# A graph convolution with a mixture of experts on one core: the loads of x placed by hand, and token gathers that run ahead by tiles

## The chip, the cores and the metric

The kernel runs on one core of one Trainium2 chip. The metric is the time of one execution in device microseconds. Each kernel is run several times, and the median is compared.

## The reference, cut to what matters

There are 12500 nodes of 256 features, 212500 edges sorted by destination (200000 drawn ones and a loop for each node), and 64 experts.

```python
h = feats * rsqrt(deg_out)[:, None]
m = segment_sum(h[src], dst, num_segments=n) * rsqrt(deg_in)[:, None]
x = (m @ W_gc + b_gc) + (feats @ W_res + b_res)
# top-2 of 64 experts: the two largest of x @ Wg + bg, softmax of the two
# each expert: gelu(tokens @ w1 + b1) @ w2 + b2, 256 -> 512 -> 256, capacity 1024
core = zeros((N, D)).at[tok].add(gate[:, None] * expert_output)
y = x + core
y = (y - mean(y, 0)) * rsqrt(var(y, 0) + eps) * gamma + beta   # over the nodes
out = layernorm(feats + y)                                      # over the features
```

## The kernel before, in words

The execution has five stretches. Up to about 400 us the degrees of the nodes are counted. Around 400 to 440 us the scaled features go to memory as h_d. From there to about 2605 us runs the graph stage: 1416 rows of up to 128 edges, each with one indirect transfer on POOL that gathers 128 rows of h_d (line L962) and one product with a 0/1 matrix on PE (L976). Work for groups of finished nodes (their products with the weights, the routing, the stores) is put into this loop at chosen rows: `at_row(t, f)` files f in a heap named todo, and after row c everything due by then is written into the program. At about 2640 us the experts begin, and they end near 3428 us. Then the batch norm and the layer norm follow, until 3577 us.

Three arrays in memory join the stages. x2_d (x_d in the trace) holds for each node its 256 features and its two gate values, and the experts gather tokens from it. z_d holds x, and the experts add their outputs to it by indirect transfers that accumulate. Afterwards the norms read z_d. The helper `by_rows` stores both: L1148 for whole groups, L1152 for the ragged end, whose source is a corner of the tile rel.

Twenty "early" tiles of tokens go through their experts inside the graph stage, on gaps of PE. `sort_early` and `early_tile` lay out their index tables, `gate_tile` writes their outputs into the tile acc, and `add_early` (L1562) adds an output to z_d. Eight of these adds (AT_ONCE) are issued right behind the last row of the graph stage, before what is left in todo; the other twelve are given to chosen parts of the experts (adds_at), where `gather` issues one in the middle of a part's gathers. Their row numbers come from at_e in the first case, and from a copy named taken_at in the second.

The experts' tokens are laid out as 73 parts of at most four tiles of 128 tokens: 219 tiles in all. `parts` is a fixed order. Some experts share an output product with their neighbour (`pair_at`). For part q:

- `begin` copies the expert's slice of the index tables (`sort_slots`, the copy L2118 and its companion), loads its weights (L1884, 1 MB) and its bias (L1886) on the queue of SP, and issues the gathers of its tokens from x2_d (L1931) on POOL.
- `turn` transposes the tokens on PE (L1947, xtp) and copies them to xT on DVE (L1951).
- `hidden` makes the first product (L1960, hp) and the gelu on ACT (L1964).
- `gates_of` (DVE) takes the gate values from the gathered rows (L1975).
- `outputs` makes the second product (L1983, yp), DVE adds the bias and scales by the gate (L1987 and L1988, yo), and POOL adds the tile to z_d (L1993).

There are 16 buffers for gathered tiles (xg), 10 for outputs (yo), 4 for weights, two for xT.

What sets the order: inside `manual_schedule` the instructions of the engines named (PE and DVE) keep the order of the program, while those of the others are placed by a scheduler. All transfers of POOL, gathers and adds, are chained in the order of the program by `in_order`. Gathers are asked for three parts ahead:

```python
if q not in pair_at and q + AHEAD < len(parts):
    begin(q + AHEAD)
if q + 1 < len(parts):
    xT = turned(q + 1)
```

The adds of one expert go to different nodes and don't wait for each other. Those of the next expert may hit the same nodes, so each waits in `landed` until every add of the group before has landed:

```python
if group != adding["group"]:
    adding.update(group=group, before=adding["these"], these=[])
for before in adding["before"]:
    tc.add_manual_dep(st.ins, before.ins.name, ...Sync...)
```

The early adds form groups of one. The final norms need x again. Its 14 pieces (LOADS, twelve of them 1 MB) are loaded on SP by the line L2151, which stands in the loop over the parts at every fourth part from part 6 on; the scheduler decides when SP issues them, as soon as their place in the tile acc is free by its reckoning, so that in the trace they start at 2030 us already. At the very end the norms load z_d (L2227) once the last add has landed.

Of the kernel before, what the change touches and what calls it, by code (L numbers as in the profile page):

```python
# [8 lines left out]
F32 = mybir.dt.float32  # L9
# [96 lines left out]
SORT_AT, TAKE_AT, STEP, AT_ONCE = 710, 796, 27, 8  # L106
# [38 lines left out]
def gnn_moe_kernel(  # L145
# [698 lines left out]
    with ExitStack() as stack:  # L844
# [274 lines left out]
        def nodes(t0, n, t):  # L1119
# [25 lines left out]
            def by_rows(to, of):  # L1145

                k = n if not last else 2
                st = [nc.sync.dma_start(  # L1148
                    to[t0 * P : (t0 + k) * P].rearrange("(t p) d -> p t d", p=P), of[:, :k]
                )]  # L1150
                if last:
                    st.append(nc.sync.dma_start(to[(t0 + k) * P : N], of[:RAG, k]))  # L1152
# [243 lines left out]
        xg_e = [xg_e, acc[:, NP + 19 * D : NP + 19 * D + D2]]  # L1396
        e_regs = {}
# [69 lines left out]
        def early_tile(i, t):  # L1467
# [20 lines left out]
            V.tensor_copy(at_e[:, :, i : i + 1], T3[:, :2, of])  # L1488
            V.tensor_copy(snd_e[:, i : i + 1], T3[:, 2, of])
# [213 lines left out]

        BATCH = 9
# [69 lines left out]
        with tc.manual_schedule(engines={  # L1774
# [18 lines left out]
            at_row(SORT_AT, sort_early)  # L1793
            at_row(TAKE_AT - 16, lambda t: soon.update(close=True))
# [38 lines left out]
    with ExitStack() as stack:  # L1833
# [33 lines left out]
        taken_at = route.tile([P, EARLY], I32)  # L1867
        V.tensor_copy(taken_at, at_e[:, 1])
# [3 lines left out]
    with ExitStack() as stack:  # L1872
# [6 lines left out]
        REGS, YO, COLS = 4, 10, RPE - 1  # L1879
        assert max(TOKENS) * TU <= COLS * P  # L1880

        def load(e):
            w = wp.tile([P, WROW], F32, name="w")
            nc.sync.dma_start(w, wpack[bass.ds(e, 1)].rearrange("a p f -> p (a f)"))  # L1884
# [35 lines left out]
        def gather(at, m, q=None):  # L1920

            xg = []
            for k in range(0, m, P):
                if k // P == -(-m // P) // 2 and q in adds_at:
                    st = add_early(adds_at[q], taken_at)
# [11 lines left out]
                in_order(i)  # L1937
                xg.append(g[:r])
# [136 lines left out]
        x_loads = LOADS[:7] + LOADS[9:] + LOADS[7:9]  # L2075
        large = [q for q in range(AHEAD, 6 + 4 * len(x_loads[:-2])) if parts[q][2] > 2 * P]
# [5 lines left out]
        def begin(q):  # L2082
            i, b, m = parts[q]
            if i not in given:
                if i not in columns_of:
                    n = 1
                    at = order.index(i)
                    while n < REGS and order[at : at + n + 1] == [*range(i, i + n + 1)]:
                        n += 1
                    _, regs = nc.values_load_multi_w_load_instructions(  # L2090
                        exp_row[0:1, i : i + n],
                        engines=[SP],
                        min_val=0,
                        max_val=E - 1,
                        skip_runtime_bounds_check_because="exp_row is an order of the experts",
                    )
                    _, columns = nc.values_load_multi_w_load_instructions(
                        exp8_row[0:1, i : i + n],
                        engines=[DVE],
                        min_val=0,  # L2100
                        max_val=(E - 1) * RPE + 1,
                        skip_runtime_bounds_check_because="exp8_row is an order of the experts",
                    )
                    for k in range(n):
                        columns_of[i + k], reg_of[i + k] = columns[k], regs[k]
                sort_slots(i, 0)
                if q >= AHEAD:
                    sort_slots(i, 1)
                given[i] = load(reg_of[i])
            xg[q] = gather(table(q), m, q)  # L2110
# [24 lines left out]
        with tc.manual_schedule(engines={mybir.EngineType.PE, DVE}):  # L2135
            for q in range(AHEAD):
                begin(q)
            V.scalar_tensor_tensor(free, node, 0.0, spread, op0=ALU.is_equal, op1=ALU.mult)
            V.tensor_tensor(slot[:, 1], free, slot[:, 0], op=ALU.add)
            for i in sorted({parts[q][0] for q in range(AHEAD)}):  # L2140
                sort_slots(i, 1)
            xT = turned(0)
            for q, (i, b, m) in enumerate(parts):
                if q >= 6 and q % 4 == 2 and (q - 6) // 4 < len(LOADS):
                    t0, n = x_loads[(q - 6) // 4]
# [7 lines left out]
                if q not in pair_at and q + AHEAD < len(parts):  # L2153
                    begin(q + AHEAD)
                if q + 1 < len(parts):
                    xT = turned(q + 1)
                mine = (*given[i], table(q), gates(q), h1, m, f"expert{i}")
                if q in pair_at:
                    rest = pair_of_outputs([kept.pop(pair_at[q]), mine])
                    begin(q + AHEAD)  # L2160
# [7 lines left out]
                else:  # L2168
                    outputs(*mine)
                if q == 16:  # L2170
# [227 lines left out]
```

## Time and profile before

| | us |
|---|---|
| three timed runs | 3569.35, 3597.57, 3601.11 |
| their median | 3597.57 |
| the profiled execution, its own time | 3578.71 |
| its span in the profile | 3576.9 |
| PE busy | 2494.7 (70%) |
| POOL busy | 2186.7 (61%) |
| DVE busy | 1797.0 (50%) |
| ACT busy | 826.2 (23%) |

The mean granted clock of PE is 0.821 over the span. The core moved 562.31 MB, 157 GB/s on the mean.

How to read it. Busy times are sums over stretches with different limits, so the share of an engine says little by itself. An instruction row gives its start, its duration in us, the engine, the line, the operation, output and inputs, and in brackets how long the engine was idle before it and what ended that idle time ("issue" where the profile shows nothing that it waited for). "SPq" rows are SP's own instructions that issue a transfer, and their duration contains the time they were held. A row of waits reads: total us, how many times, mean us. A row of groups has a count, the busy time and the mean in ns of one, then the idle time before them and what ended most of it. A row of stretches gives for each engine its busy time and its instructions, then the granted clock of PE, the share of time in which the transfer engines were busy, and GB/s.

### The profile page before, as it was taken

The page shows a single profiled execution, that of the slowest core. Times are in us where ns is not written, and L with a number is a line of the kernel's source. Part 1 is how long each engine was busy: PE and PEld are TensorE (multiplying, and loading weights), DVE is VectorE, ACT ScalarE, POOL GpSimd, SP SyncE. Part 2 cuts the span into 40 slices and gives each one's busy share as a digit, 9 for nine tenths or more (in the row PEclk, how much of TensorE's full clock was granted, in tenths as well). Part 3 has the DMA queues.
Part 4 walks back from the last instruction along what each step waited for, and adds up shares of the span by engine and source line. Part 5 has one row for each costly group of instructions (what it writes and reads, how often), then busy time and mean ns, then how long its engine had stood idle before and what let it go on. Part 6 is the DMA issues. An engine that isn't in the chain of part 4 may idle for free. (4 is left out here: it accounts for less than half of the span.)

```text
span 3576.9 us, 40976 instructions
## 1 busy us (share of the span) xinstructions
PE 2494.7 (70%) x12046; PEld 1898.2 (53%) x12121; DVE 1797.0 (50%) x7367; ACT 826.2 (23%) x2028; POOL 2186.7 (61%) x2169
## 2 busy tenths in 40 slices
PE   2626066566666667676676666578769999999966
PEld 1515033455555545555555455456547767767756
DVE  2829554255455555655455444356643333334347
ACT  1515301122112122121222112122112211211246
POOL 6270777666666666666665666666547777777621
PEclk6657567788787878788788787788889999999988
DMA  7370853455455554555554544445466667667764
GB/s 258 109 235 4 304 191 110 144 146 152 130 144 143 147 142 139 146 140 162 162 162 145 162 152 137 138 144 179 132 171 148 162 150 193 161 173 183 174 168 144
DMA packets 319779, 562.31 MB, mean 157 GB/s; under 512 B 47850, under 2 KB 236366, under 8 KB 308798
## 3 DMA queue, kind: packets, MB, share of 16 engines
q0 software_dynamic: 119456, 266.90, 29.4%
q1 hardware_dynamic: 186555, 279.83, 24.5%
q10 hardware_dynamic: 13539, 12.90, 1.2%
q8 instruction: 99, 1.62, 0.2%
q14 instruction: 130, 1.06, 0.1%
HBM read 455.41 MB, written 105.12 MB: 157 GB/s over the span
## 5 line engine op out<-in xcount | busy, mean ns | idle before, releaser
L962 POOL DMA_INDIRECT ring<-h_d,src_col x1416 | 1364.4, 964 | 748.1 <-issue 385.4
L976 PE MATMUL p<-ring,o 128*128 128x258 f32 x2832 | 899.3, 447 | 175.0 <-DMA ring<-h_d,src_col 97.1
L976 PEld LDWEIGHTS p<-ring,o 128*128 128x128 f32 x2832 | 594.7, 223 | 337.3 <-issue 148.0
L954 DVE TENSOR_SCALAR o<-lane,rel 128x128 f32<-128x128 f32 x1416 | 356.4, 298 | 328.6 <-remote 163.8
L1993 POOL DMA_INDIRECT z_d<-yo,tables x219 | 340.5, 1555 | 146.2 <-issue 48.9
L1983 PE MATMUL yp<-w,h 128*128 128x256 f32 (+7 forms) x1928 | 381.2, 392 | 9.4 <-DVE yo L1987 8.4
L1960 PE MATMUL hp<-xT,w 128*128 128x384 f32 (+22 forms) x1168 | 350.5, 454 | 2.0 <-DVE xT L1951 1.3
L1983 PEld LDWEIGHTS yp<-w,h 128*128 128x128 f32 (+7 forms) x1928 | 296.3, 174 | 71.3 <-issue 17.2
L1964 ACT ACTIVATE h<-hp,w 128x384 f32<-128x384 f32 (+21 forms) x292 | 159.1, 546 | 622.8 <-PE hp L1960 513.7
L1960 PEld LDWEIGHTS hp<-xT,w 128*128 128x128 f32 x1168 | 218.6, 192 | 112.3 <-issue 49.6
L1931 POOL DMA_INDIRECT xg<-x_d,tables x219 | 215.3, 983 | 77.9 <-issue 52.1
L1951 DVE COPY xT<-xtp 128x768 f32<-128x768 f32 (+20 forms) x73 | 63.6, 871 | 329.6 <-PE xtp L1947 295.5
L1755 ACT ACTIVATE again<-again,factor 128x256 f32<-128x256 f32 x180 | 82.4, 502 | 634.2 <-issue 364.3
L309 POOL DMA_INDIRECT early<-in_x,src_col x140 | 149.8, 1070 | 113.4 <-DMA early_d<-early 60.8
L1051 PE MATMUL q<-ident,s 128*128 128x128 f32 x236 | 58.8, 339 | 200.7 <-DVE tables L1738 72.8
L1010 ACT COPY s<-p 128x258 f32<-128x258 f32 x118 | 44.0, 373 | 636.8 <-remote 274.1
L1730 PE MATMUL q<-r_out,tables 128*128 128x98 f32 x360 | 70.1, 327 | 160.0 <-DVE tables L1738 59.0
L591 PE MATMUL deg<-o_hi,o_lo 128*128 128x98 bf16 x1254 | 105.8, 255 | 102.8 <-issue 66.0
L1987 DVE TENSOR_TENSOR yo<-yp,bb 128x256 f32<-128x256 f32 (+6 forms) x219 | 92.9, 424 | 162.5 <-PE yp L1983 132.4
L589 ACT ACTIVATE s_lo<-lane_b,nb 128x128 bf16<-128x128 bf16 x396 | 122.1, 388 | 201.6 <-PE deg_s L593 96.0
L1730 PEld LDWEIGHTS q<-r_out,tables 128*128 128x128 f32 x360 | 65.7, 238 | 177.3 <-issue 74.4
L1051 PEld LDWEIGHTS q<-ident,s 128*128 128x128 f32 x236 | 35.2, 171 | 234.4 <-DVE tables L1738 79.5
(428 smaller groups left out, 3853.0 us busy)
## 6 DMA issues: line engine op xcount, KB each, us to landing
w<-in_wpack SPq DMA_DIRECT2D x64, 1026.0 KB
again<-early_d SPq DMA_DIRECT2D x90, 256.0 KB
ring<-h_d,src_col POOLq DMA_INDIRECT x1416
acc<-in_wpack SPq DMA_DIRECT2D x20, 1026.0 KB
early_d<-early SPq DMA_DIRECT2D x70, 256.0 KB
tables<-h_d SPq DMA_DIRECT2D x104, 128.0 KB
acc<-acc_d SPq DMA_DIRECT2D x14, 896.0 KB
acc<-in_x SPq DMA_DIRECT2D x12, 1024.0 KB
```

Source lines behind the costliest of these rows:

```text
L309: GP.indirect_dma_start(out=t[:, c % 2], out_offset=None, in_=x, in_offset=bass.IndirectOffsetOnAxis(ap=src_col[:, MC + c : MC + c + 1], a ...
L589: S.activation(s_lo[:, i], lane_b, AF.Sign, bias=nb[:, k - k0, i : i + 1])
L591: T.matmul(deg, o_lo[:, i], o_hi[:, i], start=c + i == 0, stop=False)
L954: o_last[u] = V.tensor_scalar(o_of[u][:, j], lane, rel[:, c : c + 1], None, op0=ALU.is_equal)
L962: i = GP.indirect_dma_start(out=r[:, k, :D], out_offset=None, in_=h_d, in_offset=bass.IndirectOffsetOnAxis(ap=src_col[:, c : c + 1], axis=0),)
L976: i = T.matmul(p_of[g], o_of[v][:, n], r[:, k], start=j == 0, stop=j == GR - 1)
L1730: T.matmul(p_r[:, i], wide[:, i * P : (i + 1) * P], r_out, start=True, stop=True)
L1931: i = GP.indirect_dma_start(out=g[:r], out_offset=None, in_=x2_d, in_offset=bass.IndirectOffsetOnAxis(ap=at[:r, 0, k : k + 1], axis=0),)
L1960: T.matmul(hp[:, :m], w1[:, c, j * P : (j + 1) * P], xT[:, c, :m], start=c == 0, stop=c == 1,)
L1964: S.activation(h1[:, j, :m], hp[:, :m], AF.Gelu, bias=w[:, 2 * H + 4 * D + j : 2 * H + 4 * D + j + 1],)
L1983: T.matmul(yp, h1[:, j, a : a + r], w2[:, j], start=j == 0, stop=j == 3)
L1993: st = GP.indirect_dma_start(out=z_d, out_offset=bass.IndirectOffsetOnAxis(ap=at[:r, 1, k : k + 1], axis=0), in_=yo, in_offset=None, compu ...
```

## The change

It has five parts.

1. *The stores at the end of the graph stage.* Seven early adds (AT_ONCE) stand there in place of eight, so thirteen are given to parts of the experts. The late stores of z_d are declared free of a conflict with these adds, as the adds already were with the stores: the adds are a no-dep group now, and the stores name it. The adds still wait for each other.
2. *The row numbers of early tiles.* A table at_all in acc gets the row numbers of each early tile by one more copy in `early_tile` (20 in all, each with an offset from a register). It replaces at_e[:, 1] and the copy taken_at after the graph stage.
3. *The loads of x.* SP is in the manual schedule of the experts, so it keeps the order of the program there. Six pieces are loaded at chosen rows of the graph stage, four behind the last work of todo, and four in the experts, at parts 10, 20, 50 and 54.
4. *Gathers and weights.* `begin` is split: weights are loaded up to three parts ahead as before; gathers run ahead as long as the tiles from part q on fit into XG = 20 buffers (16 before), at most two parts in one call. Index tables are laid out with the gathers. The weights of the second expert wait for the first gather.
5. *Part 1.* Its tokens are transposed after the outputs of part 0, and no longer ahead of them.

In the built order of the changed kernel the matrix products and ACT's work are those of before, in the same order, but for part 5.

```diff
-SORT_AT, TAKE_AT, STEP, AT_ONCE = 710, 796, 27, 8
+SORT_AT, TAKE_AT, STEP, AT_ONCE = 710, 796, 27, 7
...
                 if soon.get("ranked", NT) <= t0 and to is z_d:
                     for i in st:
                         tc.add_to_no_dep_group("late stores", i.ins)
+                        tc.declare_no_dep(
+                            i.ins,
+                            group="early adds",
+                            reason="nodes of early tiles were ranked before",
+                        )
                         late_stores.append(i)
...
+        a = yo_at[-1] + D
+        at_all = acc[:, a : a + EARLY].bitcast(I32)
...
             V.tensor_copy(at_e[:, :, i : i + 1], T3[:, :2, of])
+            V.tensor_copy(at_all[:, i : i + 1], T3[:, 1, of])
...
+        def load_x(j):
+            t0, n = LOADS[j]
+            r = rows(t0)
+            nc.sync.dma_start(xs[:r, t0 : t0 + n], part_of(x, t0, n))
...
+            for j, r in ((9, 1090), (3, 1130), (4, 1330), (0, 1385), (1, 1390), (2, 1395)):
+                at_row(r, lambda t, j=j: load_x(j))
...
             for i in range(AT_ONCE):
+                st = add_early(i, at_all)
+                tc.add_to_no_dep_group("early adds", st.ins)
                 tc.declare_no_dep(
-                    add_early(i, at_e[:, 1]).ins,
+                    st.ins,
...
             while todo:
                 t, _, f = heapq.heappop(todo)
                 f(t)
+            for j in (5, 11, 12, 13):
+                load_x(j)
...
-        taken_at = route.tile([P, EARLY], I32)
-        V.tensor_copy(taken_at, at_e[:, 1])
...
         def load(e):
             w = wp.tile([P, WROW], F32, name="w")
-            nc.sync.dma_start(w, wpack[bass.ds(e, 1)].rearrange("a p f -> p (a f)"))
+            i = nc.sync.dma_start(w, wpack[bass.ds(e, 1)].rearrange("a p f -> p (a f)"))
+            if len(first) == 1:
+                sync(i, first[0])
+                first.append(i)
...
-                g = two.tile([P, D2], F32, name="xg", bufs=16)
+                g = two.tile([P, D2], F32, name="xg", bufs=XG)
...
-        x_loads = LOADS[:7] + LOADS[9:] + LOADS[7:9]
-        large = [q for q in range(AHEAD, 6 + 4 * len(x_loads[:-2])) if parts[q][2] > 2 * P]
+        tiles_of = [-(-m // P) for _, _, m in parts]
+        x_at = {10: LOADS[10], 20: LOADS[6], 50: LOADS[7], 54: LOADS[8]}
+        large = [q for q in range(AHEAD, 50 - AHEAD) if parts[q][2] > 2 * P]
...
+        def begin(q, which=1):
+
+            to = min(q + AHEAD, len(parts) - 1)
+            most = fetched[0] + 2 if which else AHEAD
+            while True:
+                p = fetched[0]
+                if loaded[0] <= to and (loaded[0] <= p or p >= most):
+                    i = parts[loaded[0]][0]
+                    names(i)
+                    if i not in given:
+                        given[i] = load(reg_of[i])
+                    loaded[0] += 1
+                elif p < min(most, len(parts)) and sum(tiles_of[max(q, 0) : p + 1]) <= XG:
+                    i, b, m = parts[p]
+                    names(i)
+                    if i not in laid:
+                        sort_slots(i, 0)
+                        if which:
+                            sort_slots(i, 1)
+                        laid.append(i)
+                    xg[p] = gather(table(p), m, p)
+                    fetched[0] += 1
+                elif loaded[0] > to:
+                    break
+                else:
+                    most = p
...
-        with tc.manual_schedule(engines={mybir.EngineType.PE, DVE}):
-            for q in range(AHEAD):
-                begin(q)
+        with tc.manual_schedule(engines={mybir.EngineType.PE, DVE, SP}):
+            begin(-1, 0)
...
-                if q >= 6 and q % 4 == 2 and (q - 6) // 4 < len(LOADS):
-                    t0, n = x_loads[(q - 6) // 4]
+                if q in x_at:
+                    t0, n = x_at[q]
...
-                if q not in pair_at and q + AHEAD < len(parts):
-                    begin(q + AHEAD)
-                if q + 1 < len(parts):
+                if q not in pair_at:
+                    begin(q)
+                if 0 < q < len(parts) - 1:
                     xT = turned(q + 1)
...
+                if q == 0:
+                    xT = turned(1)
```

More of the change, by code (lines that the diff above doesn't have):

```diff
@@ L1924, in gather @@
                 if k // P == -(-m // P) // 2 and q in adds_at:
-                    st = add_early(adds_at[q], taken_at)
+                    st = add_early(adds_at[q], at_all)
                     landed(st, f"early{adds_at[q]}")
@@ L1937, in gather @@
                 in_order(i)
+                if not first:
+                    first.append(i)
                 xg.append(g[:r])
@@ L2080, in gnn_moe_kernel @@
         xg, given = {}, {}
[L2082 to L2110, printed above, removed]
@@ new lines, in gnn_moe_kernel, with names @@
+        loaded, fetched = [0], [0]
+        def names(i):
+            if i in columns_of:
+                return
+            n = 1
+            at = order.index(i)
+            while n < REGS and order[at : at + n + 1] == [*range(i, i + n + 1)]:
+                n += 1
+            _, regs = nc.values_load_multi_w_load_instructions(
+                exp_row[0:1, i : i + n],
+                engines=[SP],
+                min_val=0,
+                max_val=E - 1,
+                skip_runtime_bounds_check_because="exp_row is an order of the experts",
+            )
+            _, columns = nc.values_load_multi_w_load_instructions(
+                exp8_row[0:1, i : i + n],
+                engines=[DVE],
+                min_val=0,
+                max_val=(E - 1) * RPE + 1,
+                skip_runtime_bounds_check_because="exp8_row is an order of the experts",
+            )
+            for k in range(n):
+                columns_of[i + k], reg_of[i + k] = columns[k], regs[k]
```

8 lines of the change are left out of this document (5 added, 3 removed).

## The prediction

> **What bounds the kernel now.** I read the stretches of the span first, because the change touches only the hand-over from the graph stage to the experts and the experts themselves.
>
> ```profile
> span 3576.9 us, 40976 instructions
> core 0: us, PE busy (x) PEld busy (x) DVE busy (x) ACT busy (x) POOL busy (x), PEclk, DMA share, GB/s
> 2640.00:2720.00 80.00, 78.80 (x408) 61.04 (x409) 29.76 (x92) 19.00 (x37) 48.33 (x38) 0.97 0.65 162
> 2720.00:3280.00 560.00, 531.57 (x2489) 392.06 (x2489) 208.40 (x684) 110.78 (x203) 409.38 (x321) 0.98 0.70 168
> 3280.00:3440.00 160.00, 148.47 (x636) 109.80 (x634) 56.37 (x172) 32.11 (x56) 109.04 (x84) 0.98 0.65 146
> ```
>
> The experts run from about 2640 to 3440 us. In the middle 560 us PE is busy 95% at a granted clock of 0.98, so matrix work sets the pace and only 28 us are idle there. POOL is nearly as full: 409.4 us busy, and behind each of its 321 indirect transfers stands a gap of 0.30 us (rows below), another 96 us. That leaves POOL 54 us of real waiting in 560. Two engines are close to full, and PE's idle time is what a better order could win.
>
> ```profile
> PE xtp L1947 <- DMA xg<-x_d,tables: 18.2, 17, 2.4
> PE yp L1983 <- DVE yo L1987: 8.4, 3, 3.2
> PE hp L1960 <- DVE xT L1951: 1.3, 1, 1.3
> ```
>
> These are PE's waits between 2640 and 3430 us: 18.2 us for gathered tokens (xg, late 17 times), 8.4 us for DVE's outputs. Then the hand-over, from the lists in order of time on SP, POOL, DVE and PE:
>
> ```profile
> 2601.28 15.33 SPq L2151 DMA_DIRECT2D acc<-in_x  x2
> 2623.01 0.37 SPq L1148 DMA_DIRECT2D z_d<-rel  x1
> 2625.36 0.44 SPq L1152 DMA_DIRECT2D x_d<-rel  x1
> 2628.51 0.37 SPq L1884 DMA_DIRECT2D w<-in_wpack  x1
> 2584.99 1.87 POOL L1562 DMA_INDIRECT z_d<-acc,rel  x1 [0.30 <-issue]
> 2612.36 1.55 POOL L1562 DMA_INDIRECT z_d<-acc,rel  x1 [3.01 <-DMA z_d<-acc,rel]
> 2616.39 1.71 POOL L1562 DMA_INDIRECT z_d<-acc,rel  x1 [2.47 <-DMA z_d<-acc,rel]
> 2629.35 1.02 POOL L1931 DMA_INDIRECT xg<-x_d,tables  x1 [11.25 <-issue]
> 2609.64 0.15 DVE L1268 SCALAR_TENSOR_TENSOR rel<-src_col 128x3 f32<-128x3 f32 x1
> 2618.24 0.20 DVE L1864 CAST exp_row<-ord_p 1x64 int32<-1x64 f32 x1
> 2621.12 0.17 DVE L2118 COPY tables<-tables 128x7 int32 x1
> 2637.94 0.66 PE L1947 MATMUL xtp<-ident,xg 128*128 128x128 f32 x2 [18.81 <-issue]
> 2640.57 4.79 PE L1960 MATMUL hp<-xT,w 128*128 128x176 f32 x16 [0.66 <-DMA bb<-in_b]
> ```
>
> The first gather starts at 2629.35, though its index table is copied at 2621.29 and the last token rows (rel) are complete at 2609.79. What is late is their store: SP is held from 2601 to 2616.6 by two loads of x (the second waits for the early adds, which run one after another on POOL), the store of z_d then waits for the eighth add, and the x_d store follows at 2625.36. The gather starts 4.0 us after that issue, the first weights 3.2 us after it. PE stands still for 18.8 us.
>
> **The change part by part.** Durations are those of the profiled execution: its span is 3576.9 us and its own time 3578.71 us, 1.8 us around the span. The three timed runs are 3569.35, 3597.57 and 3601.11 us, median 3597.57; the profiled execution is 18.9 us under it.
>
> *Start.* In the built order of the changed kernel the x_d store stands ahead of the last x loads on SP, the z_d store no longer waits for the adds, and seven adds stand ahead of the gathers instead of eight. The store can go at about 2610 and has landed by 2614 (4.0 us, as above); the seventh add ends at 2613.9 (2612.36 + 1.55). The table at 2621.3 is then what comes last: the gather starts about 2621.5, 7.9 us earlier. The first weights need exp_row (2618.4); with the 3.2 us that now lie between the x_d store and them they go at 2619 to 2622, also some 7 to 9 us earlier. Besides, the second expert's weights now wait for the first gather. Today gather 1 ends on POOL at 2630.37 and PE starts at 2637.94: 7.6 us, with four weight loads and two x loads in flight; an early add with little beside it had landed 2.5 to 3.0 us after its end (the idle times of the L1562 rows). So 0 to 4.6 us more. I take 2 of it, because one weight load stays beside the gather: **-10 us**, between -5 (weights held by something the trace doesn't show) and -12.5.
>
> *Part 0.* The transposes of part 1 now stand behind part 0's outputs, so DVE's copy of 1024 columns is no longer covered:
>
> ```profile
> 2645.19 1.04 PE L1947 MATMUL xtp<-ident,xg 128*128 128x128 f32 x8
> 2646.27 1.23 DVE L1951 COPY xT<-xtp 128x1024 f32<-128x1024 f32 x1 [5.42 <-PE xtp L1947]
> 2646.07 3.75 PE L1983 MATMUL yp<-w,h 128*128 128x256 f32 x16
> ```
>
> Today 3.75 us of yp hide that copy; the four transposes cost the same in either place. **+1.3**, between 0 and 2.3 (the transposes too).
>
> *Gathers further ahead.* 20 buffers in place of 16; counted in the two built orders, when an add is issued the tokens of on average 17 tiles are gathered before it instead of 11. No gather and no add is saved. 18.2 us of PE waits could go. Whether they do depends on POOL, which must still do everything, and on this rule of the program: the adds of one expert wait until those of the expert before have landed.
>
> ```profile
> 3365.26 1.62 POOL L1993 DMA_INDIRECT z_d<-yo,tables  x1 [1.08 <-DVE yo L1988]
> 3369.08 1.49 POOL L1993 DMA_INDIRECT z_d<-yo,tables  x1 [0.30 <-DVE tables L2118]
> 3377.31 1.62 POOL L1993 DMA_INDIRECT z_d<-yo,tables  x1 [2.87 <-DVE yo L1987]
> 3418.16 1.59 POOL L1993 DMA_INDIRECT z_d<-yo,tables  x1 [3.00 <-DVE gate L1975]
> 3421.92 1.55 POOL L1993 DMA_INDIRECT z_d<-yo,tables  x1 [0.30 <-issue]
> 3426.67 1.55 POOL L1993 DMA_INDIRECT z_d<-yo,tables  x1 [3.19 <-DMA z_d<-yo,tables]
> ```
>
> With three gathers between, an expert's adds end at 3370.57 and the next expert's begin at 3377.31: 6.7 us, while weights stream in. Near the end, without weights, it is 3.2 us (3423.47 to 3426.67). The label of 3377.31 names DVE, but those outputs were long ready; I read it as a landing. Three adds take 3 x 1.87 = 5.6 us, so such a part costs POOL 5.6 + 6.7 = 12.3 us, more than PE's 11.2 us for it (the hp, xtp and yp matmuls of three tiles, from 3400.37 to 3411.54 in the rows below). Hence POOL's chain of adds and landings paces much of the stage, and gathers moved ahead only leave its gaps. PE then stops at full yo buffers (10) instead of at missing tokens. I take **-3** of the 18.2, between 0 and -18.2.
>
> ```profile
> 3400.37 5.32 PE L1960 MATMUL hp<-xT,w 128*128 128x384 f32 x16
> 3405.53 0.82 PE L1947 MATMUL xtp<-ident,xg 128*128 128x128 f32 x6
> 3406.19 5.35 PE L1983 MATMUL yp<-w,h 128*128 128x256 f32 x24
> 3424.71 3.76 PE L1983 MATMUL yp<-w,h 128*128 128x256 f32 x16
> L1562 POOL DMA_INDIRECT z_d<-acc,taken_at x12 | 19.2, 1604 | 21.0 <-DMA z_d<-yo,tables 15.3 <-issue 5.8
> ```
>
> The Trainium skill, "DMA: Bandwidth & Descriptors", section "Anatomy of one DMA", gives about 2.0 us plus the bytes at 436 GB/s: 2.3 us, an estimate, for an add of 128 rows of 1 KB. The trace shows 3.2 to 6.7; by the page's figure the landings would be covered by three gathers and all 18.2 us would go (second case below). The Trainium skill, "Perfetto Trace Analysis", section "What DMA-bound means", says that where the issuing engine's sequencer is the limit, larger descriptors are what matters; by it no reordering wins anything here, this term is 0 and the sum 3 us worse.
>
> *One add moves* from the hand-over into the experts: 1.60 + 0.30 us and 21.0/12 = 1.75 us of waiting on POOL, **+2**, between 0 (in POOL's slack) and 3.7.
>
> *Tail.* From the chain that ended last:
>
> ```profile
> 3436.83 3.84 DMA z_d<-yo,tables
> ...
> 3443.46 2.94 SPq L2227
> ```
>
> PE ends at 3428.47 (3424.71 + 3.76) and z_d is complete only at 3440.67 (3436.83 + 3.84): 12.2 us. In the new order the last 20 indirect transfers are adds alone; without weights a part then costs 5.6 + 3.2 = 8.8 us against PE's 11, so POOL can catch up by some 6 us, or, if it enters with ten tiles waiting, need 10 x 1.87 + 3 x 3.2 = 28 us, 16 more than now. I take **-2**.
>
> *Graph stage.* Twenty copies into at_all with a register offset, 0.17 us each and 0.34 us of issue (the second L2118 row of this kind below): 10 us of DVE. DVE is half idle there, **+1**, at most 10. Ten x loads stand at chosen rows or behind the last of them. What they wait for on SP now:
>
> ```profile
> 2621.64 0.17 DVE L2118 COPY tables<-tables 128x7 int32 x1 [0.34 <-issue]
> SPq L2151 <- PE bank L1204: 31.9, 4, 12.0
> SPq L2151 <- DMA z_d<-acc,rel: 14.3, 3, 8.5
> ```
>
> The 31.9 us delay nobody whom I could find: the stores behind them wait longer for their own data. Three loads now come within ten rows; at 2.9 us for 1 MB (the row of L2227 above, a z load of the same size) they hold the transfers for 9 us, covered by the ring of 20 gathered rows. **0**, up to +9 without that cover.
>
> Sum: -10 + 1.3 - 3 + 2 - 2 + 1 = **-10.7, say -11 us**. On its own time: 3578.7 - 11 = 3568. As the profiled execution lies low among the runs, I set the forecast against the middle of all four times, 3586.7: **3576 us**. On the median it would be 3587.
>
> **The rivals.**
> 1. *PE's waits all go* (POOL has room enough). For it: 54 us of POOL waiting in the middle stretch, and deeper prefetch is what a late gather wants. Against: 12.3 us per part above. All 18.2, and 6 in the tail: -11 - 15 - 4 = -30, 3557 us.
> 2. *Adds fall behind* (the other side). The new order has nine changes of expert without a gather between, three before. At 6.7 us of landing, three gathers (3 x (1.02 + 0.30) = 4.0 us) that used to fill it are missing: 6 x 4.0 = 24 us more, -11 + 24 = +13, 3600 us. It decides if landings stay above 5.4 us (11 - 5.6) there. For it: the 6.7 us. Against: six of those changes lie at the end, where weights have stopped and 3.2 us was seen.
> 3. *The start doesn't move*: the first weights or the gather wait for something else, so the change doesn't do what it says. -11 + 10 = -1, 3586 us. For it: the first weight load waits for many things in the built order. Against: all that I can place are over by 2619.
>
> **How the numbers follow.** Forecast 0.55, first rival 0.22, second 0.15, third 0.08. About 1% (36 us) is what a measurement of this kernel can tell from no change, as its runs spread over 32 us. Half of the first rival, with a gain in the graph stage, passes -36: 0.12, and 0.01 of the forecast, 0.13 faster. Half of the second with the +16 tail: 0.08, and 0.02 elsewhere, 0.10 slower. The rest, 0.77, is within 1%. The range goes from the first rival less 10 to the second plus 5, since runs of one kernel lie up to 17 us from the middle I set against: 3547 to 3605.
>
> **What would show it.** Right: the first gather near 2621.5 and the first hp near 2630; the L1947 waits below 5 us; waits of yp for yo grown to 10 us or more; POOL's busy time unchanged within 3 us. Wrong: L1947 waits gone and yp waits not grown (first rival); z_d complete more than 15 us after PE's last yp (second); the first gather after 2626 (third).

## The result and the profile after

The changed kernel takes 3613.93 us (median of 22 runs, 3584.27 to 3635.28), the one before 3587.73 us (22 runs, 3564.41 to 3609.29) on the same chip: a ratio of 1.0061, with a 95% interval of 1.004 to 1.0082. It is 26 us slower, and the forecast was 11 us faster. The profiled execution of the changed kernel has a span of 3612.1 us, 35 us over the one before.

The start of the experts came out nearly as worked out. Its rows after the change, behind one row of before (PE's L1863, which became L1882) that marks the end of routing:

```profile
2614.39 0.79 PE L1863 MATMUL ord_p<-perm,pos 64*1 64x64 f32 x6 [4.94 <-DVE src_col L1315]
```

```profile
2634.46 0.79 PE L1882 MATMUL ord_p<-perm,pos 64*1 64x64 f32 x6 [4.78 <-DVE src_col L1320]
2639.69 0.36 SPq L1903 DMA_DIRECT2D w<-in_wpack  x1
2642.30 1.12 POOL L1953 DMA_INDIRECT xg<-x_d,tables  x1 [11.93 <-DVE tables L2168]
2647.90 4.39 PE L1984 MATMUL hp<-xT,w 128*128 128x176 f32 x16 [0.66 <-issue]
2657.99 0.41 ACT L1988 ACTIVATE h<-hp,w 128x176 f32<-128x176 f32 x1 [3.90 <-remote]
2664.99 7.13 PE L1984 MATMUL hp<-xT,w 128*128 128x512 f32 x16 [1.39 <-DVE xT L1975]
```

Routing ended 20.1 us later in this execution. From there the first gather takes 7.8 us (15.0 before) and the first hp 13.4 us (26.2 before), so 12.7 us are won at the start. ACT stood still for several us in part 0 (3.90 us ahead of its row above; "remote" is a release that the profile can't place), which put the second part's hp at 17.1 us behind the first (9.2 before).

Then the experts lose it. PE's waits there, with one of DVE's; before, PE waited 18.2 us for tokens and 8.4 us for outputs:

```profile
PE yp L2007 <- DVE yo L2011: 36.7, 17, 5.1
PE xtp L1971 <- DMA xg<-x_d,tables: 2.8, 2, 1.7
DVE yo L2011 <- DMA z_d<-yo,tables: 99.5, 32, 10.1
```

Tokens are no longer late. But DVE waits 99.5 us for an add to land before it may write an output buffer (yo), and PE behind it. That row was 1.7 us before:

```profile
DVE yo L1987 <- DMA z_d<-yo,tables: 1.7, 2, 0.9
```

The stretch from the first gather to the end of the last add, both kernels, before first (columns as in the table of stretches in the prediction):

```profile
2629.00:3441.00 812.00, 760.03 (x3534) 563.49 (x3534) 294.59 (x947) 161.89 (x295) 574.97 (x450) 0.97 0.68 164
```

```profile
2642.00:3476.00 834.00, 762.56 (x3534) 564.17 (x3534) 293.39 (x953) 161.69 (x295) 574.30 (x451) 0.96 0.67 161
```

POOL does the same work in 22 us more: its busy time is 575.0 and 574.3 us. What grew is its idle time ahead of adds, from 98.0 to 120.9 us by its rows (without the 0.30 us that stand behind each transfer). And the tail grew: PE's last yp ends at 3456.04, the last add is in place at 3476.02.

```profile
3452.28 3.76 PE L2007 MATMUL yp<-w,h 128*128 128x256 f32 x16
```

```profile
3472.10 3.92 DMA z_d<-yo,tables
```

These are 20.0 us in place of 12.2. From the end of routing, the stretches give 22 us more from the first gather on and 7 us less ahead of it, 15 us in all. The interval of the measured 26 us goes from 14 to 29 us, so whether the other 11 us are more than noise isn't shown.

### The profile page after: what moved, and what is told of

Read it like the earlier page. It is cut to its first block, busy times and chain, and to the rows that moved or that the text cites. A ratio compares the mean times of both kernels' runs of the same rounds, so it can differ in the third digit from the quotient of the medians.

```text
span 3612.1 us, 41020 instructions
## 1 busy us (share of the span) xinstructions
PE 2499.9 (69%) x12046; PEld 1904.0 (53%) x12121; DVE 1795.3 (50%) x7386; ACT 825.0 (23%) x2028; POOL 2181.7 (60%) x2169
## 5 line engine op out<-in xcount | busy, mean ns | idle before, releaser
L2007 PE MATMUL yp<-w,h 128*128 128x256 f32 (+7 forms) x1928 | 385.0, 390 | 42.3 <-DVE yo L2011 36.7
```

The lines of the kernel that those rows point to most:

```text
L2007: T.matmul(yp, h1[:, j, a : a + r], w2[:, j], start=j == 0, stop=j == 3)
```

## The experiments

They ran on other chips than the first comparison; on most, the stages ahead of the experts take some 480 us less (the kernel before: 3087 to 3090 us), while the experts take as long as here (the changed kernel: 831.2 us here, 831.7 us there). So each ratio is to the kernel before on the same chip, and stretches of the experts are compared directly. "Experts" below is the time from the start of the first gather to the end of the last add's instruction: 808.9 us before, 831.2 after. Each comes from one profiled execution. Two executions of one kernel gave 831.2 and 831.7 us, two of another, on two chips, 776.4 and 764.2, so a difference of a few us between two of these figures shows little.

**Is it the distance, the rest of the change, or the place of the gathers?** Four kernels. *near* gathers as before:

```diff
-            most = fetched[0] + 2 if which else AHEAD
+            most = min(q + AHEAD + 1, len(parts)) if which else AHEAD
-                elif p < min(most, len(parts)) and sum(tiles_of[max(q, 0) : p + 1]) <= XG:
+                elif p < min(most, len(parts)):
```

with XG = 16.

> The changed kernel with the gathers of before: part q+3 is gathered in part q, 16 buffers; the stores, the x loads, the table and the late transposes of part 1 stay changed. Theory 1 (adds follow each other across experts with no gather between, so the landing of one group stands bare on POOL, and POOL's chain is what ends the experts): POOL's idle time between two adds falls from 36.9 us to about 12, the stretch from the first gather to the last add from 831 to about 809 us, PE's waits of yp for yo from 42 to under 20 us (about 8 of them in part 0), and the time is 20 to 25 us under the changed kernel, so 5 to 10 under the one before. Theory 2 (the distance itself costs, gathers stand ahead of adds): the same here. Theory 3 (the x loads or the order on SP cost the experts their 20 us): the stretch stays at 825 to 831 us and the time within 8 us of the changed kernel.

Measured: 3082.64 us against 3089.67, ratio 0.9974 (0.9959 to 0.9989). Experts 804.0 us. PE's waits for outputs are gone and those for tokens are back:

```profile
PE xtp L1971 <- DMA xg<-x_d,tables: 32.0, 28, 4.2
```

Without the new distance the change is a gain of 7 us. Theory 3 is out. The second part's hp comes 10.7 us after the first here (2157.78 less 2147.12), with the same start as in the changed kernel, and 10.0 to 12.0 us in the other traces of this start from such chips. In *far_tied2* below, which has this start too and ran on a chip of the first kind, it comes 16.2 us after:

```profile
2582.51 4.64 PE L1987 MATMUL hp<-xT,w 128*128 128x176 f32 x16 [0.66 <-DVE xT L1978]
2598.69 9.61 PE L1987 MATMUL hp<-xT,w 128*128 128x512 f32 x16 [5.72 <-DVE xT L1978]
```

So the 17.1 us don't belong to one execution alone: both traces of this start on such a chip have them, and why is open.

*far* is the kernel before with only the split `begin`, 20 buffers and `begin(q)` in place of `begin(q + AHEAD)`.

> The kernel before with only the new gathers: by tiles, up to 20 buffers, two parts in a call; hand-over, x loads and early adds as before. Theories 1 and 2: first gather to last add about 825 to 831 us (809 before), idle between adds 30 us or more, waits of xtp for xg under 5 us; the time 15 to 22 us over the kernel before. Theory 3: 805 to 812 us, and no slower than before.

Measured: ratio 1.0078 (1.0055 to 1.01), experts 830.2 us. The new gathers alone make the whole loss, and more, as the better start is missing. Its waits are those of the changed kernel:

```profile
PE yp L1983 <- DVE yo L1987: 36.0, 14, 5.7
```

The stretches of *near* and *far*, near first:

```profile
2141.00:2946.00 805.00, 761.43 (x3534) 561.47 (x3534) 296.89 (x954) 162.17 (x295) 575.41 (x451) 0.98 0.70 167
```

```profile
2144.00:2976.00 832.00, 762.66 (x3534) 565.62 (x3534) 294.29 (x947) 161.99 (x295) 572.64 (x450) 0.96 0.68 160
```

*even* spreads the gathers tile by tile:

```diff
+            left = [tiles_of[q - 1] + (q % 2) if which else 99]
...
-                elif p < min(most, len(parts)) and sum(tiles_of[max(q, 0) : p + 1]) <= XG:
+                elif p < min(most, len(parts)) and left[0] > 0 and (
+                    sum(tiles_of[max(q, 0) : p]) + got[0] + 1 <= XG
+                ):
...
-                    xg[p] = gather(table(p), m, p)
-                    fetched[0] += 1
+                    xg.setdefault(p, []).extend(gather(table(p), m, p, got[0]))
+                    left[0] -= 1
```

> The changed kernel with 20 buffers as there, but the gathers go tile by tile: in part q as many tiles as part q-1 had, one more in every second part, so that gathers stand between nearly all groups of adds while the distance is about 17 tiles. Theory 1: idle between two adds falls to about 15 us, first gather to last add to 810 to 816 us, and the time is 12 to 20 us under the changed kernel. Theory 2: the distance stays, so 826 to 831 us and the time within 5 us of the changed kernel.

Measured: ratio 1.0037 (1.0021 to 1.0052), experts 825.9 us. Idle between two adds of token tiles fell from 36.9 to 21.0 us, but 10.7 us turned up ahead of three early adds that now follow another add with no gather between, and PE still waits for outputs:

```profile
PE yp L2009 <- DVE yo L2013: 43.4, 17, 6.7
```

Of the 21.0 us, 20.2 stand at the six changes of group in the tail, where there is no gather left to put between. So ahead of adds that follow another add directly, POOL is idle for 31.7 us here and 36.9 in the changed kernel, and the experts gained as much, 5.3 us. The run moved little of what theory 1 names, and doesn't refute it.

*nowait* leaves out the wait of the second expert's weights for the first gather (the three lines with `first` in `load`).

> The changed kernel without the wait of the second expert's weights for the first gather. If that wait pushes the weights into the time at which ACT fetches its code in part 0 (ACT stood still from 2651.5 to 2658.0 us there), the gap goes: the second part's first hp comes 9 us after the first one's, as before, in place of 17, and the time falls by 4 to 8 us. If the gathers are what delays ACT, the gap stays at 15 to 17 us, the first hp comes 2 to 4 us later than now, and the time is the same or up to 4 us longer.

Measured: ratio 1.0042 (1.0022 to 1.0063), experts 820.4 us. The second part's hp comes 10.0 us after the first, but in *near*, with the wait, it comes 10.7 us after. The first hp comes 18.1 us after the end of routing instead of 13.4. The wait is worth these 4 to 5 us at the start; the whole time shows no difference that could be measured.

**The changed kernel again, and 16 buffers.**

> The changed kernel once more, beside the next three. If the 26 us between the two kernels are the experts' (20) and the tail's (8) less what the start gains (4 to 12), it stands 12 to 24 us over the kernel before here too, with 826 to 831 us from the first gather to the last add, and the 6 us that ACT stood still in part 0 are there only if they belong to the kernel. If the graph stage is slower for the change, its rings take over 10 us longer than in the runs of the two kernels near and even, which have the same graph stage.

Measured: ratio 1.0055 (1.0028 to 1.0082), experts 831.7 us, no stop of ACT in part 0. The graph stage, first to last gather of h_d, in *far* (the graph stage of before) and here:

```profile
264.09 0.94 POOL L962 DMA_INDIRECT ring<-h_d,src_col  x1 [2.27 <-issue]
...
2097.65 0.95 POOL L962 DMA_INDIRECT ring<-h_d,src_col  x1 [0.30 <-issue]
```

```profile
268.77 0.94 POOL L962 DMA_INDIRECT ring<-h_d,src_col  x1 [4.21 <-DMA h_d<-acc]
...
2102.65 0.94 POOL L962 DMA_INDIRECT ring<-h_d,src_col  x1 [0.30 <-issue]
```

From start to start these are 1833.6 and 1833.9 us. The other ten traces of the changed graph stage on such chips lie between 1834.7 and 1841.9 us, so the copies into at_all and the placed x loads cost 0 to 8 us there, by the single trace of the stage of before. On chips of the first kind it is 2176.0 us before, and 2198.5 and 2181.8 (*far_tied2*) with the changed stage.

*mid* is the changed kernel with XG = 16.

> The changed kernel with 16 buffers in place of 20, still by tiles and two parts in a call (a distance of about 13 to 14 tiles). If the distance sets the loss: first gather to last add between near (804) and the changed kernel (831), 812 to 820 us, and the tail 9 to 14 us. If it is the rule by tiles and not the distance: 826 us or more, as with 20. If four more buffers alone cost: 804 to 808.

Measured: ratio 1.0096 (1.0064 to 1.0129), experts 845.0 us, the slowest of all. The second case (826 us or more) allows that, though it hadn't the 14 us over the changed kernel. At an add the tokens of 13.4 tiles are gathered ahead on the mean (17.3 in the changed kernel), so the loss doesn't follow the distance. With 16 buffers the rule by tiles issues the gathers in lumps, 15 changes of group have none between (10 in the changed kernel), and both waits come at once, PE's for tokens and POOL's for landings:

```profile
PE xtp L1971 <- DMA xg<-x_d,tables: 49.6, 32, 5.7
POOL z_d L2017 <- DMA z_d<-yo,tables: 67.1, 20, 8.0
```

**What makes the landings late.** In the changed kernel, the queue of SP and POOL side by side at two changes of group:

```profile
3012.47 0.33 SPq L1903 DMA_DIRECT2D w<-in_wpack  x1
```

```profile
2955.67 1.62 POOL L1570 DMA_INDIRECT z_d<-acc  x1 [0.97 <-DMA z_d<-yo,tables]
2957.60 0.98 POOL L1953 DMA_INDIRECT xg<-x_d,tables  x1 [0.30 <-PE yp L2007]
2958.88 0.93 POOL L1953 DMA_INDIRECT xg<-x_d,tables  x1 [0.30 <-PE hp L1984]
2960.11 1.41 POOL L2017 DMA_INDIRECT z_d<-yo,tables  x1 [0.30 <-issue]
...
3012.50 1.50 POOL L2017 DMA_INDIRECT z_d<-yo,tables  x1 [0.30 <-issue]
3014.30 1.01 POOL L1953 DMA_INDIRECT xg<-x_d,tables  x1 [0.30 <-issue]
3015.62 0.98 POOL L1953 DMA_INDIRECT xg<-x_d,tables  x1 [0.30 <-PE hp L1984]
3021.61 1.62 POOL L2017 DMA_INDIRECT z_d<-yo,tables  x1 [5.02 <-DVE yo L2011]
```

Both times two gathers stand between. At 2957 the add had landed within 2.8 us and POOL went on at once. At 3014 a weight load had been issued at the same moment as the add, and the next group started 7.6 us after its end. The label names DVE, but by DVE's rows that output had been ready for 33 us. The records of single transfers show it too: the 112 rows of this add (its tile is not full) moved from 3017.2 to 3020.4 us, amid the weights' 1 MB, which moved from 3013.7 to 3019.8. The add issued 1.9 us before it moved from 3012.8 to 3014.0.

I then took all changes of group of each kernel outside the tail (ahead of the last gather, 71 to 73), and from the records of transfers the share of the 5 us around the end of the last add (1 us before it to 4 us behind it, each transfer counted where it starts) in which SP's queue kept the transfer engines busy. "Heavy" is half or more. With little of such traffic (under a tenth), a change costs POOL 0.1 to 0.6 us of idle time, in every kernel. Heavy ones: 17 with 48.7 us idle before, 16 with 49.3 in near; 24 with 64.4 in the changed kernel (26 with 75.0 in its repeat), 21 with 73.2 in far, 25 with 66.9 in even. That is 2.7 to 3.5 us each time, and the far-running kernels have more of them.

The sum by place says something else as well. Of POOL's 98.0 and 120.9 us of idle time ahead of adds, 78.3 before and 80.6 after stand at changes outside the tail that have a gather between: more of them are heavy after the change, but fewer have a middle traffic. What is new stands where one group follows another with no gather between: 15.1 us at four such changes outside the tail, where there was none before, and 18.9 us at six in the tail, where three had 8.3. One of each in the changed kernel:

```profile
2776.01 1.47 POOL L2017 DMA_INDIRECT z_d<-yo,tables  x1 [0.30 <-DVE yo L2011]
2782.48 1.56 POOL L2017 DMA_INDIRECT z_d<-yo,tables  x1 [5.00 <-DVE yo L2012]
...
3447.88 1.56 POOL L2017 DMA_INDIRECT z_d<-yo,tables  x1 [0.30 <-issue]
3452.39 1.56 POOL L2017 DMA_INDIRECT z_d<-yo,tables  x1 [2.95 <-DMA z_d<-yo,tables]
```

So I take it that the gathers had stood in the waits for landings and covered them, as theory 1 has it. The experts fit, in the order of the number of such changes: 804.0 us with 3 (near), 825.9 with 9 (even, early adds counted), 831.2 with 10 (the changed kernel; 820.4 in nowait), 845.0 with 15 (mid). No run fills these changes alone and leaves the rest, so this part is argued and not shown.

*far_now* and *near_now* take the weights away:

```diff
         def load(e):
+            if len(held) >= 4 and "over" not in issued:
+                held.append(held[len(held) - 4])
+                return held[-1]
```

> The changed kernel, but weights and biases are loaded for the first four experts only, and the later ones use those again. Theory A (adds land late while weights stream, and far-running gathers shift the adds into that time: 2.6 us of idle at a change of expert then, 0.3 without): POOL's idle at changes falls from 97 us to under 35 outside the tail, first gather to last add to 755 to 780 us, and the same as near_now within 5 us. Theory B (the distance itself makes POOL late): still 15 to 20 us longer than near_now, with yo buffers full.

> The kernel near, with weights and biases loaded for the first four experts only. Theory A: first gather to last add 755 to 780 us, within 5 us of far_now. Theory B: 15 to 20 us under far_now.

Measured: 3030.65 and 3032.76 us, ratios 0.9814 (0.9778 to 0.985) and 0.9827 (0.9789 to 0.9864). Experts 750.9 and 756.2 us. far_now first:

```profile
2139.00:2892.00 753.00, 741.59 (x3534) 555.86 (x3534) 296.62 (x954) 161.94 (x295) 574.63 (x451) 0.99 0.50 84
```

```profile
2137.00:2895.00 758.00, 742.57 (x3534) 555.92 (x3534) 295.46 (x953) 161.91 (x295) 575.25 (x451) 0.99 0.50 83
```

Theory A holds in this: without weights there is no loss. POOL issues the same transfers at the same 575 us, PE hardly waits, and the long distance is no worse (5 us better by the stretches, 2 us by the medians, within their intervals), where it was 27 us worse. The weight streams cost the near kernel 48 us and the far one 80 us. Some 20 us of that are PE's own: its busy time falls from 761.4 and 762.6 us to 742.6 and 741.6, and its granted clock rises from 0.98 and 0.96 to 0.99. POOL's idle time ahead of adds falls from 92.5 to 45.0 us and from 120.9 to 40.2. Of these 40.2 us, 28.4 stand at the ten changes with no gather between, as many as in the changed kernel, and do no harm: the adds run 17.5 us behind their outputs (median) in place of 26.5, and PE is idle for 11 us only. So the streams are needed for the loss, and so is the new order of the gathers: neither makes the 27 us alone. That a later add meets more of the weights, the second half of theory A, is a count (17 against 24 heavy changes) and no more, as the sum of idle time at changes with a gather between hardly differs.

**Weights at another moment.** If the streams are the price, only their time needs to move. Each weight load also waits for the landing of a group of adds, the moment at which POOL begins the next one:

```diff
+            if str(adding["group"]).startswith("expert"):
+                for st in adding["these"]:
+                    sync(i, st)
```

> The kernel near, but each weight load also waits until the newest group of adds ahead of it in the program has landed, which is the moment at which POOL begins the next group: 1 MB then streams while that group's adds are issued, and its last add should land when the stream is over. Theory A (landings under a weight stream are POOL's price): idle at changes with heavy traffic falls from 49 us to 15 to 30, first gather to last add from 804 to 770 to 790 us, the time 10 to 30 us under near. Theory A', the traffic matters but a stream tied to one landing only meets the next one (adds of one or two tiles are issued in 2 to 4 us, the stream needs 3 to 5): idle stays at 40 us or more and the time within 6 us of near. If weights come too late for PE, hp waits for w and the time rises.

> The changed kernel with the same tie of weight loads to landings. Its adds run 25 to 35 us behind the outputs, so a load comes when PE is only about one part away from needing it. Theory A: idle at changes with heavy traffic falls from 64 to 75 us to under 45, first gather to last add from 831 to 785 to 810 us, the time 10 to 25 us under the changed kernel. Against it: hp waits for w (more than 20 us in all), and the time is no better than the changed kernel's.

Measured: near_tied 1.0017 (1.0002 to 1.0032), worse than near; far_tied 0.9948 (0.9932 to 0.9964). In near_tied there are 18 heavy changes with 52.7 us, about as in near, as theory A' said, but its time rose by some 13 us over near's. PE's waits for tokens grew by 12 us, from 32.0 in near; why the gathers come later wasn't followed up:

```profile
PE xtp L1974 <- DMA xg<-x_d,tables: 43.7, 24, 5.0
```

In far_tied heavy changes fell to 11 with 33.5 us, the waits for outputs went, and PE waits for weights instead:

```profile
PE hp L1987 <- DMA w<-in_wpack: 29.2, 11, 7.7
```

*far_tied2* ties to the group one earlier (`adding["before"]` in place of `adding["these"]`), *near_tied2* does so in near.

> far_tied with the tie one group earlier: a weight load waits for the landing of the group before the newest one, so it comes about one part (11 us) sooner and still starts where POOL begins a group. If the 31.5 us in which PE waited for weights in far_tied are only their lateness: these waits fall under 8 us, idle at changes with heavy traffic stays at 30 to 50 us (33.5 in far_tied, 75 in the changed kernel), and the time is 5 to 20 us under far_tied. If the landing waits come back with the earlier loads (60 us or more at heavy traffic), the tie has lost its phase and the time is between far_tied and the changed kernel.

> The same kernel as far_tied2, once more. From its trace (experts from the second part's start to the last add 755 us, against 788 in the kernel before and 808 to 814 in the changed one; start 3 to 11 us shorter than before) it should stand 30 to 45 us under the kernel before. The 20 us measured on a chip with runs 55 us apart would then be that spread. If it stands 15 to 22 us under it again, the profiled execution was a lucky one, and its experts take over 765 us here.

> The kernel near (gathers three parts ahead, 16 buffers) with the weight loads tied to the landing of the group before the newest, as in far_tied2. If the timing of the weights alone gives the gain: idle at changes with heavy traffic under 20 us, PE's waits for tokens under 12 us (31.6 in near), and the time within 6 us of far_tied2. If the far gathers are needed as well: PE still waits over 20 us for tokens, and the time is 12 us or more over far_tied2.

Measured: far_tied2 0.996 (0.9928 to 0.9993) on a chip of the first kind, 3532.73 against 3552.63 us, with runs 57 us apart; and 0.9872 (0.9854 to 0.989) in its repeat, 3046.85 against 3089.36 us. near_tied2 0.9901 (0.9886 to 0.9917), 3058.66 us. Experts 776.4, 764.2 and 781.0 us. Heavy changes are 4, 5 and 5 with 7.6, 9.2 and 15.1 us. So the waits at heavy traffic fell further than expected of far_tied2, and near_tied2 lies between its two cases: idle at heavy traffic is gone, part of the waits for tokens is left. The repeat of far_tied2, its stretch and PE's waits in it:

```profile
2143.00:2909.00 766.00, 744.95 (x3534) 556.76 (x3534) 296.81 (x954) 162.37 (x295) 575.32 (x451) 0.99 0.73 175
```

```profile
PE hp L1987 <- DMA w<-in_wpack: 5.6, 1, 5.6
PE xtp L1974 <- DMA xg<-x_d,tables: 0.6, 1, 0.6
```

and near_tied2's:

```profile
PE xtp L1974 <- DMA xg<-x_d,tables: 18.1, 15, 3.4
```

The timing of the weights is worth the larger part (near_tied2 stands some 23 us under near, far_tied2 some 57 under the changed kernel), and with it the far gathers are worth another 12 us. far_tied2 beats both kernels: 42 us under the one before, and, by the repeat's ratio against 1.0055, 1.8% under the changed one. On the chip of the first kind it is 20 us under the one before; why less there is open.

## Why the prediction was wrong, point by point

*Start, -10 us.* Right, and just beyond the far end of its range: 12.7 us at the first hp. The first gather comes 7.1 us earlier (7.9 forecast), and from there to the first hp it takes 5.6 us less (2 forecast, of at most 4.6). *nowait* puts 4 to 5 of these down to the wait of the second expert's weights.

*Part 0, +1.3.* Right on the chips of the experiments: the second part's hp comes 10.0 to 12.0 us after the first, 9.3 in far, which has the order of before. On chips of the first kind it comes 17.1 and 16.2 us after, 9.2 before: +7 to +8, outside the range, and the cause is open.

*Graph stage, +1.* It fits on the chips of the experiments (0.3 to 8.3 us over one trace of the stage of before). On the first chip the two profiled executions differ there by some 20 us; whether that is the spread of the stage or the change isn't shown.

*One add moves, +2.* No waiting came of it: POOL's idle time ahead of the early adds in the experts, worked out from their rows, is 17.4 us with twelve and 12.2 with thirteen.

*Tail, -2.* Wrong in sign: +7.8 (20.0 against 12.2). POOL did enter with many outputs waiting, as the upper bound (+16) had it: the last 20 adds run 18.9 us behind their outputs (median), 12.0 before. It comes from the far gathers too, for in near the last add ends 4.0 us after PE's last yp, in the changed kernel 17.5.

*Gathers further ahead, -3, between 0 and -18.2.* This is the step that failed. The 18.2 us of waits for tokens went, as the whole of the range allowed. But the term is +27 us by the experts of near and of the changed kernel (804.0 and 831.2, the tail included), and +21 by those of the kernel before and of far (808.9 and 830.2), where -5 had been set down with the tail. The text had POOL's chain of adds and landings right as what paces the stage, and that PE would stop at full yo buffers: waits for outputs rose from 8.4 to 36.7 us. What it had wrong is that gathers moved ahead "only leave its gaps". They had filled these gaps, the waits for landings, and with them gone the waits stand bare: POOL's idle time ahead of adds rose by 22.9 us, and what is new of it stands at changes of group with no gather between, ten in place of three. POOL paces the stage only while the weights stream and make landings outside the tail long; without the streams the far gathers cost nothing. The range left out that the chain itself could grow.

*The second rival, 3600 us at 0.15*, had the side, the size and the place. It forecast 24 us for bare changes of group, and idle time between adds did rise by 25.2 us (11.7 to 36.9), 14.6 of them outside the tail and 10.6 in it. It counted nine such changes; POOL's rows have ten. Its condition, landings above 5.4 us, was met at one of the ten (2.7 to 5.6 us from an add's end to the next group's start), and the loss came all the same, so that 24 and 25.2 us agree is in part luck. It was refuted for the reason "six of those changes lie at the end, where weights have stopped and 3.2 us was seen", but 2.9 to 4.4 us were seen there at each, and POOL was too far behind to hide them. The first rival was right that the waits for tokens go, and wrong that nothing takes their place; the third, that the start doesn't move, is out by the rows of the start.

The Trainium skill, "DMA: Bandwidth & Descriptors", section "Anatomy of one DMA", gave an estimate of 2.3 us for an add of 131 KB. Where no weights stream, the rows of the tail show somewhat more (2.9 us at the least from an add's end to the next group's start), and under a stream 7.6 us; the measurement decides. The Trainium skill, "Perfetto Trace Analysis", section "What DMA-bound means", was taken to say that no reordering wins anything here. The Trainium skill speaks there of an issuing engine whose track is filled with transfers, and POOL's was not: in the changed kernel it stood idle for 120.9 us ahead of adds. far_tied2, with the same transfers, stands some 57 us under the changed kernel by the moment of its loads alone.

## What to carry to other kernels

A prefetch that removes a wait also moves work away from where it stood, here gathers out of the waits for landings; before taking the wait as a gain, ask what the moved work was covering, and price each landing by the traffic at its time. Where an engine waits for small transfers to land, time the large ones: tie a bulk load to the landing, so that it streams while the next small ones are still being issued, and leave it enough lead. To find whether an order or a collision costs, take the traffic away in both versions; their difference vanished here (from +27 to -5 us in the stretch, with -5 no more than two executions of one kernel can differ by).

## What was not expected of the hardware

One 1 MB load beside an add of 112 rows of 1 KB made its landing last 7.6 us from the end of its instruction, where an add of 128 such rows took under 2.8 us alone. The streams' price was 48 to 80 us over 64 experts, with the transfer engines busy only 0.67 to 0.70 of the time. The chips differ by some 480 us in the stages ahead of the experts and hardly in the experts. With the weights' traffic PE's busy time was some 20 us longer, at a granted clock of 0.96 to 0.98 in place of 0.99; in near the clock covers about half of that, by its ratio, in the changed kernel all of it. Whether the waits or the traffic lowered the clock was not tried.
